# A graph layer's sorting stage: node products added by VectorE from PSUM instead of by GpSimd, the bias added by a matmul later

## The chip, the core and the metric

The kernel runs on one core of a Trainium2 chip. The metric is device time in microseconds. Five engines work in parallel, each through its own in-order queue: TensorE (PE in the profile; its weight loads are the row PEld), VectorE (DVE), ScalarE (ACT), GpSimd (POOL) and SyncE (SP, which only issues DMAs here). They wait for each other by semaphores.

## What is computed

Four steps, each added to the running `x` of 6250 nodes by 256 features:

```
x = x + gnn0(layernorm(x), src, dst, edge_weight)
x = x + ffn0(layernorm(x))          # 8 experts, all used, weighted by a softmax
x = x + gnn1(layernorm(x), src, dst, edge_weight)
x = x + ffn1(layernorm(x))          # 32 experts, one per node

gnn0:  h   = x @ weight_l
       agg = segment_sum(edge_weight[:, None] * h[dst], src)   # 100000 edges
       out = agg + bias_l + x @ weight_r + bias_r
```

The change is in gnn0. The node's own product `x @ weight_r` and the two biases have nothing to do with the edges; `h` is stored and gathered by edge.

## The kernel before, in words

The nodes lie in 49 tiles of 128 rows, and `X` (128 x 49 x 256, f32) holds the running `x` on chip throughout. The program has three stages.

**The sorting stage** (lines 385 to 591, the first 390 us). The edges come sorted by `dst`, but gnn0 sums by `src`. So they are sorted on chip, in 25 groups of 32 edges per partition. The loop at the end of the excerpt below runs over the groups. `count_group(g)` compares each edge's tile number with all 49 (`hot`, DVE), and PE counts by triangular matrices into `count`; ACT copies that into `start`. `place_group(g)` works out each edge's place (DVE: `same`, `picked`, `pos`, `place_b`), makes one-hot rows `to` (L523) and payloads `loads`: four slices by DVE (L527), the fifth by ACT in 32 small instructions (L502), here called pieces. 32 matmuls then move the payloads to their places (`put`, L530); ACT copies `put` to `there` (L533), and POOL assembles `Z` from it with five small instructions. `settle_group(g)` carries the counts to the next group (L482 to L488).

The node products ride along, two tiles per group. `center0` takes mean and variance on DVE, the square root and the centering on ACT (`xn`). `products0` turns `xn` on PE, ACT copies the turned tile to `nT` (L341), and one product of 512 columns gives both `x @ weight_l` and `x @ weight_r` in one PSUM bank `ph` (L570). ACT copies both halves, scaled, to `hs` (L571). A DMA of SP stores the left half as `h0`; POOL adds the right half to `X` (L572), and then the bias (L573).

**Layer 0** (to about 1850 us) interleaves the gather and sum of gnn0 (`aggregate0`: 18 columns of edges per tile; POOL's indirect DMA L201, ACT and DVE weight the rows, L230 and L231, PE sums them in `acc`, L701, DVE adds both halves of `acc` to `X`, L704) with ffn0. **Layer 1** does the same for gnn1 and ffn1, with line L277 as its sum and the one-hot rows of L222 made from `dl_c`, the edge list's local destinations.

Within a stage the order of each engine's queue is not written out: a planner of the framework fixes it when the program is built, from the order in the source, the dependencies and its own idea of durations. `tc.issue_after(ins)` makes the instructions in its block come behind `ins` on the same engine. Buffers limit how far an engine can run ahead: `loads`, `to`, `put`, `ph` and `hs` have two each, `hot` three.

Two biases and their sum: `bias0` (L190 to L192) is loaded by two DMAs on ACT's queue and summed by POOL, in the source before the iotas that make POOL's tables (L430 to L446).

Of the kernel before, what the change touches and what calls it, by code (L numbers as in the profile page):

```python
# [49 lines left out]
def gnn_ffn_kernel(ctx: ExitStack, tc: tile.TileContext, a, out):  # L50
# [56 lines left out]

    src_c = const.tile([P, NCOL], I32, name="src_c")
    val_c = const.tile([P, NCOL], F32, name="val_c")
    dl_c = const.tile([P, NCOL], F32, name="dl_c")  # L110

    bads = [const.tile([P, 1], F32, name=f"bad{i}") for i in range(2)]
    badis = [const.tile([P, 1], I32, name=f"badi{i}") for i in range(2)]
# [73 lines left out]
    wlr = early.tile([P, 2, 2, D], F32, name="wlr")  # L187
    nc.scalar.dma_start(wlr[:, :, 0, :], a["L0_gnn_weight_l"].rearrange("(k p) d -> p k d", p=P))
    nc.scalar.dma_start(wlr[:, :, 1, :], a["L0_gnn_weight_r"].rearrange("(k p) d -> p k d", p=P))
    bias0 = across("L0_gnn_bias_l", early)  # L190
    bias0r = across("L0_gnn_bias_r", early)
    nc.gpsimd.tensor_add(bias0, bias0, bias0r)  # L192
    bias1 = across("L1_gnn_bias")
    br0 = across("L0_ffn_br")
    br1 = across("L1_ffn_router_b")
# [249 lines left out]
    sizes = early.tile([P, NT, NG], F32, name="sizes")  # L445
    nc.gpsimd.memset(ZJ[:, :, NG], 0.0)  # L446

    def count_group(g):


        cs = slice(g * GC, (g + 1) * GC)
        tg = tb[:, cs].rearrange("p (b c) -> p b c", c=4)
        hot = early.tile([P, CB, NT, 4], BF, tag="hot", name="hot", bufs=3)
        nc.vector.tensor_tensor(hot, tg[:, :, None, :].to_broadcast([P, CB, NT, 4]),
                                which_t[:, None, :, :].to_broadcast([P, CB, NT, 4]), OP.is_equal)

        four = early.tile([P, 4, NT, 4], BF, tag="four", name="four", bufs=1)
        nc.vector.tensor_tensor(four, hot[:, :4], hot[:, 4:], OP.add)
        mine = early.tile([P, 4, NT, 2], BF, tag="mine", name="mine", bufs=2)
        nc.vector.tensor_tensor(mine, four[:, :, :, :2], four[:, :, :, 2:], OP.add)  # L460

        count = psum.tile([P, 4, NT], F32, tag="count", name="count", bufs=1)
        base = base_of.pop()
        nc.tensor.matmul(count, row, base[:, None, :].to_broadcast([P, 4, NT]), start=True, stop=True,
                         skip_group_check=True)
        for i in range(2):
            nc.tensor.matmul(count, tri, mine[:, :, :, i], start=False, stop=True, skip_group_check=True)
            for u in range(3):
# [3 lines left out]
        nc.scalar.activation(start, count[:, :, :, None].to_broadcast([P, 4, NT, 4]), AF.Copy)  # L472
        for i in range(2):
            nc.tensor.matmul(count[:, 3, :], rest_tri, mine[:, 3, :, i], start=False, stop=True, skip_group_check=True)
# [13 lines left out]
        nc.vector.scalar_tensor_tensor(full_of[0], total, float(P), full, op0=OP.is_ge, op1=OP.add)  # L488
        nc.gpsimd.tensor_sub(sizes[:, :, g], total, base)

    def place_group(g, hot, start):

        cs = slice(g * GC, (g + 1) * GC)

# [4 lines left out]
        nc.vector.tensor_tensor(same, same, ahead[:, None].to_broadcast([P, 4, 8, 8]), OP.mult)  # L499
        loads = early.tile([P, NPAY, CB, NT, 4], BF, tag="loads", name="loads", bufs=2)  # L500
        for c in range(GC):
            nc.scalar.activation(loads[:, NPAY - 1, c // 4, :, c % 4], hot[:, c // 4, :, c % 4], AF.Copy,  # L502
                                 scale=last[:, g * GC + c:g * GC + c + 1])
# [34 lines left out]
        nc.gpsimd.tensor_add(some[:, 1], there[:, 2], there[:, 3])  # L538
        nc.gpsimd.tensor_add(Z[:, 1, :, g], some[:, 1], there[:, 4])

    def center0(tiles):

        n = len(tiles)
        mv = work.tile([P, NB, 2], F32, tag="mv", name="mv")
        for j, t in enumerate(tiles):
            st = work.tile([P, 6], F32, tag="st", name="st", bufs=4)
            nc.vector.bn_stats(st, X[:, t, :])
            nc.vector.bn_aggr(mv[:, j, :], st)
        std = work.tile([P, NB], F32, tag="std", name="std", bufs=3)
        nc.vector.tensor_scalar(std[:, :n], mv[:, :n, 1], LN_EPS, None, op0=OP.add)  # L550
        shift = work.tile([P, NB], F32, tag="shift", name="shift")
        nc.vector.tensor_scalar(shift[:, :n], mv[:, :n, 0], -1.0, None, op0=OP.mult)
        nc.scalar.activation(std[:, :n], std[:, :n], AF.Sqrt)
        xn = early.tile([P, 2, D], F32, tag="xn0", name="xn0", bufs=2)
        for j, t in enumerate(tiles):
            nc.scalar.activation(xn[:, j, :], X[:, t, :], AF.Identity, bias=shift[:, j:j + 1])
        return tiles, xn, std

    def products0(tiles, xn, std):

        n = len(tiles)
        rstd = work.tile([P, NB], F32, tag="rstd0", name="rstd0")
        nc.vector.reciprocal(rstd[:, :n], std[:, :n])
        hs = early.tile([P, 2, 2, D], F32, tag="hs", name="hs", bufs=2)
        for j, t in enumerate(tiles):
            nT = early.tile([P, 2, P], F32, tag="nT", name="nT", bufs=2)
            transposed(psum, xn[:, j, :], nT)
            ph = psum.tile([P, 2, D], F32, tag="mm", name="ph", bufs=2)
            for k in range(2):
                nc.tensor.matmul(ph, nT[:, k, :], wlr[:, k], start=(k == 0), stop=(k == 1))  # L570
            nc.scalar.activation(hs[:, j], ph, AF.Copy, scale=rstd[:, j:j + 1])  # L571
            nc.gpsimd.tensor_add(X[:, t, :], X[:, t, :], hs[:, j, 1, :])  # L572
            nc.gpsimd.tensor_add(X[:, t, :], X[:, t, :], bias0)  # L573
# [61 lines left out]
    with tc.tile_pool(name="layer0", bufs=1) as wp, tc.tile_pool(name="outs0", bufs=1, side="right") as wo_pool, \  # L635
# [56 lines left out]
        def aggregate0():  # L692
            for b, tiles in enumerate(blocks0):
                idx, dl, w = edges[b]
                for i, t in enumerate(tiles):
                    acc = psum.tile([P, 2, D], F32, tag="agg", name="acc", bufs=2)
                    for j in range(EW):
                        if j % SJ == 0:
                            s = one_hots(wp, dl[:, i, :], j, 3)
                        m = weighted(wp, h0, idx[:, i, j:j + 1], w[:, i, j:j + 1], 12, 6)  # L700
                        nc.tensor.matmul(acc, s[:, j % SJ, :], m, start=(j == 0), stop=(j == EW - 1))  # L701
                        if j == EW - 1:
                            for half in range(2):
                                nc.vector.tensor_add(X[:, t, :], X[:, t, :], acc[:, half, :])  # L704
                        yield
# [404 lines left out]
```

## Time and profile before

| what | value |
|---|---|
| median of 3 runs | 2901.26 us (2896.87 to 2902.55) |
| the profiled execution | 2895.13 us, its span 2893.4 us |
| busy, whole span | PE 93%, DVE 70%, POOL 67%, ACT 56% |
| granted PE clock, whole span | 0.974 |
| POOL's L572, 49 instructions | 78.9 us, mean 1611 ns |
| POOL's L573, 49 instructions | 52.0 us, mean 1060 ns |
| ACT's L571, 49 instructions of 128x512 | 33.7 us, mean 687 ns |
| ACT's L502, 800 instructions | 206.4 us, mean 399 ns |

A line such as L572 is line 572 of the kernel. In a group row the columns are line, engine, operation, names written and read, shapes, count, then busy time and mean, then the idle time of the engine before these instructions and what ended it. In a timeline the columns are start and duration in us. Consecutive instructions of one engine overlap in the record: the time that one really costs its engine is better read from its start to the next start than from its duration.

### The profile page before, as it was taken

Reading aid. Unit: us, or ns where it says so; the run is one execution under the profiler, and the core shown is the slowest. Engines: PE = TensorE matmul, PEld = TensorE weight load, DVE = VectorE, ACT = ScalarE, POOL = GpSimd, SP = SyncE. Lnnn points to the kernel's source line nnn. Section 1 sums busy time; section 2 is a strip of 40 time slices with the busy share of each in tenths; the row PEclk is TensorE's granted clock in tenths of the full one; section 3 lists DMA queues with packets and bytes.
Section 4 is the critical chain, followed back from the end, with each engine's and each line's share of the span. In section 5 each row is a group of like instructions: output and inputs, shape, how many; then the busy total and the mean of one; then the engine's idle time right before and its main releaser. Section 6 shows DMA issues by size and latency. Waiting matters only on the chain.

```text
span 2893.4 us, 37030 instructions
## 1 busy us (share of the span) xinstructions
PE 2677.7 (93%) x10336; PEld 1750.2 (60%) x10336; DVE 2012.4 (70%) x4917; ACT 1626.1 (56%) x3790; POOL 1926.1 (67%) x1932
## 2 busy tenths in 40 slices
PE   5888848888999999999999998779999999999998
PEld 2444427665566666666666665556666666666666
DVE  8999977778768767766566555666666666666630
ACT  6777737655555555555555545455555555555532
POOL 4666667777767676766675527677777777777720
PEclk9999978999999999999999999999999999999999
DMA  4000043333333333333332214333333333333310
GB/s 150 19 19 19 19 141 97 101 100 102 92 99 95 90 101 97 91 100 96 91 102 82 78 39 135 109 108 103 107 108 109 106 108 102 108 106 109 109 44 12
DMA packets 123140, 260.73 MB, mean 90 GB/s; under 512 B 32236, under 2 KB 68904, under 8 KB 122920
## 3 DMA queue, kind: packets, MB, share of 16 engines
q0 software_dynamic: 79872, 218.21, 26.2%
q1 hardware_dynamic: 31672, 32.42, 3.4%
q10 hardware_dynamic: 11376, 7.60, 0.8%
q8 instruction: 85, 1.39, 0.2%
q14 instruction: 135, 1.11, 0.1%
HBM read 238.87 MB, written 19.25 MB: 89 GB/s over the span
## 4 chain that ended last, share of the span: by engine, by line
PE 65%; DVE 17%; DMA 8%; issue 4%; ACT 4%; POOL 1%; ACTq 0%; POOLq 0%; DVEq 0%
PE ph L748 19%; PE py L760 10%; PE py L1000 9%; PE ph L984 9%; PE acc L701 6%; PE acc L277 4%; DMA g<-h,src_c 4%; DMA g<-h,idx 3%; DVE loads L527 3%; DVE to L523 2%; DVE m L231 2%; ACT m L230 2%; PE ph L987 1%; PE ph L214 1%; POOL g L201 1%
## 5 line engine op out<-in xcount | busy, mean ns | idle before, releaser
L201 POOL DMA_INDIRECT g<-h,idx x882 | 903.1, 1024 | 391.8 <-DVE m L231 175.2
L201 POOL DMA_INDIRECT g<-h,src_c x718 | 725.6, 1011 | 227.8 <-issue 104.2
L230 ACT ACTIVATE m<-g,w 128x256 fp32r<-128x256 f32 x882 | 394.7, 500 | 260.0 <-PE acc L701 136.0
L751 ACT ACTIVATE hT<-ph,shift,scale 128x512 f32<-128x512 f32 (+3 forms) x480 | 329.0, 696 | 314.6 <-PE ph L748 313.4
L230 ACT ACTIVATE m<-g,val_c 128x256 fp32r<-128x256 f32 x718 | 349.7, 503 | 273.6 <-PE acc L277 132.2
L231 DVE SCALAR_TENSOR_TENSOR m<-g,val_c,m 128x256 fp32r<-128x256 f32 x718 | 337.1, 483 | 211.2 <-ACT m L230 207.6
L231 DVE SCALAR_TENSOR_TENSOR m<-g,w,m 128x256 fp32r<-128x256 f32 x882 | 397.7, 476 | 42.5 <-ACT m L230 41.4
L748 PE MATMUL ph<-nT,w 128*128 128x512 f32 (+3 forms) x960 | 373.1, 524 | 25.0 <-ACT hT L751 24.8
L760 PE MATMUL py<-wo,hT 128*128 128x256 f32 x1568 | 382.1, 387 | 13.8 <-DVE X L762 10.5
L1000 PE MATMUL py<-w,hm 128*128 128x256 f32 x1568 | 386.7, 385 | 3.1 <-ACT hm L989 3.1
L701 PE MATMUL acc<-m,s 128*128 128x512 f32 x882 | 341.4, 490 | 38.0 <-DVE scale L657 24.7
L984 PE MATMUL ph<-nT,w 128*128 128x512 f32 (+2 forms) x832 | 374.8, 571 | 0.0
L748 PE MATMUL ph<-hT,w 128*128 128x512 f32 (+3 forms) x960 | 368.5, 518 | 0.5 <-ACT hT L751 0.5
L760 PEld LDWEIGHTS py<-wo,hT 128*128 128x128 f32 x1568 | 294.7, 193 | 80.8 <-DVE X L762 26.9
L277 PE MATMUL acc<-m,s 128*128 128x512 f32 x782 | 332.2, 499 | 1.7 <-DVE m L231 1.7
L1000 PEld LDWEIGHTS py<-w,hm 128*128 128x128 f32 x1568 | 292.1, 193 | 52.9 <-ACT hm L989 4.6
L222 DVE TENSOR_TENSOR s<-col,dl 128x384 fp32r<-128x384 f32 x294 | 161.4, 551 | 187.0 <-PE acc L701 184.8
L748 PEld LDWEIGHTS ph<-nT,w 128*128 128x128 f32 x960 | 175.2, 195 | 174.2 <-issue 118.1
L989 ACT ACTIVATE hm<-ph,b 128x512 f32<-128x512 f32 (+2 forms) x208 | 136.8, 659 | 200.0 <-PE ph L987 199.6
L748 PEld LDWEIGHTS ph<-hT,w 128*128 128x128 f32 x960 | 176.2, 193 | 118.9 <-issue 88.3
L701 PEld LDWEIGHTS acc<-m,s 128*128 128x128 f32 x882 | 169.7, 195 | 109.8 <-issue 48.9
L984 PEld LDWEIGHTS ph<-nT,w 128*128 128x128 f32 x832 | 157.2, 191 | 101.5 <-issue 81.1
(248 smaller groups left out, 3359.0 us busy)
## 6 DMA issues: line engine op xcount, KB each, us to landing
g<-h,idx POOLq DMA_INDIRECT x882, 2.8
g<-h,src_c POOLq DMA_INDIRECT x718, 2.8
h<-hs SPq DMA_DIRECT2D x25, 256.0 KB, 2.1
X<-in_x_dram SPq DMA_DIRECT2D x12, 512.0 KB, 8.9
out_dram<-o SPq DMA_DIRECT2D x11, 512.0 KB, 3.4
h<-hs SPq DMA_DIRECT2D x9, 512.0 KB, 3.0
w<-in_L_ffn_W_dram ACTq DMA_DIRECT2D x2, 2048.0 KB, 11.2
wo<-in_L_ffn_Wo_dram ACTq DMA_DIRECT2D x1, 2048.0 KB, 20.0
```

What stands on the lines that cost most here:

```text
L201: nc.gpsimd.indirect_dma_start(out=g, out_offset=None, in_=h, in_offset=bass.IndirectOffsetOnAxis(ap=idx, axis=0))
L222: nc.vector.tensor_tensor(s[:, :n], col[:, None, :].to_broadcast([P, n, P]), dl[:, j:j + n, None].to_broadcast([P, n, P]), OP.is_equal)
L230: nc.scalar.activation(m[:, 0, :], g, AF.Copy, scale=w)
L231: nc.vector.scalar_tensor_tensor(m[:, 1, :], g, w, m[:, 0, :], op0=OP.mult, op1=OP.subtract)
L277: nc.tensor.matmul(acc, s[:, (j - js.start) % SJ, :], m, start=opens, stop=done)
L701: nc.tensor.matmul(acc, s[:, j % SJ, :], m, start=(j == 0), stop=(j == EW - 1))
L748: nc.tensor.matmul(ph[:, :nw], (w1, w2)[layer][:, e, k, m * P:(m + 1) * P], src[:, k, :nw], start=(k == 0), stop=(k == 1))
L751: nc.scalar.activation(hT[:, m, :nw], ph[:, :nw], AF.Relu, bias=shift[:, layer, c:c + 1], scale=scale[:, layer, c:c + 1])
L760: nc.tensor.matmul(py, hT[:, k, j * P:(j + 1) * P], wo[:, e, k, :], start=(k == 0), stop=(k == 1))
L984: nc.tensor.matmul(ph[:, :nw], w1f[:, k, c * P:(c + 1) * P], nT[:, k, :nw], start=(k == 0), stop=False)
L989: nc.scalar.activation(hm[:, :nw], ph[:, :nw], AF.Relu, bias=b1[:, c:c + 1])
L1000: nc.tensor.matmul(py[:, j, :], now[:, cols], w2f[:, c, :], start=False, stop=(c == NC1 - 1), skip_group_check=True)
```

## The change

The right half of a product is no longer evicted by ACT. DVE multiplies it, in PSUM, by the reciprocal deviation and adds it to `X` in one instruction; ACT evicts only the left half, so `hs` has half its size. POOL's two additions per tile are gone. The bias is added in layer 0: on `acc`, behind the first of a tile's 18 products, a further product of `ones_b` (three rows of ones, else zero) and `bias0_b` (the bias split in three bf16 parts on those rows). POOL makes these behind its tables. The mean and variance of a group's tiles (`stats0`) are taken one group earlier than before, and the reciprocal moves from `products0` to `center0`. In `place_group` the pieces 16 to 31 are made to follow ACT's last eviction of `products0` of the same group. `dl_c` becomes bf16 (its values are 0 to 127, or those plus 8192).

```diff
-    dl_c = const.tile([P, NCOL], F32, name="dl_c")
+    dl_c = const.tile([P, NCOL], BF, name="dl_c")
...
-    bias0 = across("L0_gnn_bias_l", early)
-    bias0r = across("L0_gnn_bias_r", early)
-    nc.gpsimd.tensor_add(bias0, bias0, bias0r)
+    bias0 = across("L0_gnn_bias_l", prep)
+    bias0r = across("L0_gnn_bias_r", prep)
...
     nc.gpsimd.memset(ZJ[:, :, NG], 0.0)
 
+    nc.gpsimd.tensor_add(bias0, bias0, bias0r)
+    bias0_b = const.tile([P, D], BF, name="bias0_b")
+    nc.gpsimd.memset(bias0_b, 0.0)
+    ones_b = const.tile([P, P], BF, name="ones_b")
+    nc.gpsimd.memset(ones_b, 0.0)
+    for i in range(3):
+        own = slice(32 * i, 32 * i + 1)
+        nc.gpsimd.memset(ones_b[own, :], 1.0)
+        for _ in range(i):
+            nc.gpsimd.tensor_copy(bias0_b[own, :], bias0[own, :])
+            nc.gpsimd.tensor_sub(bias0[own, :], bias0[own, :], bias0_b[own, :])
+        nc.gpsimd.tensor_copy(bias0_b[own, :], bias0[own, :])
...
-    def place_group(g, hot, start):
+    def place_group(g, hot, start, evicted):
...
         for c in range(GC):
-            nc.scalar.activation(loads[:, NPAY - 1, c // 4, :, c % 4], hot[:, c // 4, :, c % 4], AF.Copy,
-                                 scale=last[:, g * GC + c:g * GC + c + 1])
+
+            with ExitStack() as behind:
+                for ins in evicted[-1:] if c >= GC // 2 else ():
+                    behind.enter_context(tc.issue_after(ins.ins))
+                nc.scalar.activation(loads[:, NPAY - 1, c // 4, :, c % 4], hot[:, c // 4, :, c % 4], AF.Copy,
+                                     scale=last[:, g * GC + c:g * GC + c + 1])
...
-    def center0(tiles):
+    def stats0(tiles):
...
         nc.scalar.activation(std[:, :n], std[:, :n], AF.Sqrt)
+        return tiles, std, shift
+
+    def center0(tiles, std, shift):
+
+        n = len(tiles)
+        rstd = work.tile([P, NB], F32, tag="rstd0", name="rstd0")
+        nc.vector.reciprocal(rstd[:, :n], std[:, :n])
         xn = early.tile([P, 2, D], F32, tag="xn0", name="xn0", bufs=2)
         for j, t in enumerate(tiles):
             nc.scalar.activation(xn[:, j, :], X[:, t, :], AF.Identity, bias=shift[:, j:j + 1])
-        return tiles, xn, std
-
-    def products0(tiles, xn, std):
+        return tiles, xn, rstd
+
+    def products0(tiles, xn, rstd):
...
-            nc.scalar.activation(hs[:, j], ph, AF.Copy, scale=rstd[:, j:j + 1])
-            nc.gpsimd.tensor_add(X[:, t, :], X[:, t, :], hs[:, j, 1, :])
-            nc.gpsimd.tensor_add(X[:, t, :], X[:, t, :], bias0)
-        nc.sync.dma_start(h0[tiles[0] * P:(tiles[0] + n) * P, :].rearrange("(t p) d -> p t d", p=P), hs[:, :n, 0, :])
+            evicted.append(nc.scalar.activation(hs[:, j], ph[:, 0, :], AF.Copy, scale=rstd[:, j:j + 1]))
+            nc.vector.scalar_tensor_tensor(X[:, t, :], ph[:, 1, :], rstd[:, j:j + 1], X[:, t, :],
+                                           op0=OP.mult, op1=OP.add)
+        nc.sync.dma_start(h0[tiles[0] * P:(tiles[0] + n) * P, :].rearrange("(t p) d -> p t d", p=P), hs[:, :n, :])
+        return evicted
...
     counted = count_group(0)
-    centered = center0(pairs[0])
+    measured = stats0(pairs[0])
+    centered = center0(*measured)
+    measured = stats0(pairs[1])
     settle_group(0, *counted[2:])
     for g in range(NG):
...
-        products0(*tiles0)
-        place_group(g, *now[:2])
+        evicted = products0(*tiles0)
+        place_group(g, *now[:2], evicted)
         if g + 1 < NG:
-            centered = center0(pairs[g + 1])
+            centered = center0(*measured)
+            if g + 2 < NG:
+                measured = stats0(pairs[g + 2])
             settle_group(g + 1, *counted[2:])
...
                         nc.tensor.matmul(acc, s[:, j % SJ, :], m, start=(j == 0), stop=(j == EW - 1))
+                        if j == 0:
+                            nc.tensor.matmul(acc[:, 0, :], ones_b, bias0_b, start=False, stop=False,
+                                             skip_group_check=True)
```

More of the change, by code (lines that the diff above doesn't have):

```diff
@@ L550, in center0 @@
         nc.vector.tensor_scalar(std[:, :n], mv[:, :n, 1], LN_EPS, None, op0=OP.add)
-        shift = work.tile([P, NB], F32, tag="shift", name="shift")
+        shift = work.tile([P, NB], F32, tag="shift", name="shift", bufs=3)
         nc.vector.tensor_scalar(shift[:, :n], mv[:, :n, 0], -1.0, None, op0=OP.mult)
         nc.scalar.activation(std[:, :n], std[:, :n], AF.Sqrt)
+        return tiles, std, shift
[3 more added lines that the diff above has]
+        nc.vector.reciprocal(rstd[:, :n], std[:, :n])
         xn = early.tile([P, 2, D], F32, tag="xn0", name="xn0", bufs=2)
@@ L556, in center0 @@
             nc.scalar.activation(xn[:, j, :], X[:, t, :], AF.Identity, bias=shift[:, j:j + 1])
-        return tiles, xn, std
-    def products0(tiles, xn, std):
+        return tiles, xn, rstd
+    def products0(tiles, xn, rstd):
         n = len(tiles)
-        rstd = work.tile([P, NB], F32, tag="rstd0", name="rstd0")
-        nc.vector.reciprocal(rstd[:, :n], std[:, :n])
-        hs = early.tile([P, 2, 2, D], F32, tag="hs", name="hs", bufs=2)
+        hs = early.tile([P, 2, D], F32, tag="hs", name="hs", bufs=2)
+        evicted = []
         for j, t in enumerate(tiles):
```

## The prediction

> **What bounds the kernel now.** I read the table of busy time by stretch first, to find the stage that the change touches and its limit. Columns: stretch, length, busy us (and instructions) of PE, PE's weight load, DVE, ACT and POOL, granted clock, DMA share, GB/s.
>
> ```profile
> 82.90:368.40 285.50, 249.29 (x1100) 126.91 (x1101) 285.14 (x622) 226.97 (x840) 183.76 (x200) 1.00 0.06 19
> 450.00:1850.00 1400.00, 1342.40 (x4922) 885.01 (x4921) 986.16 (x2499) 793.09 (x1558) 944.69 (x925) 0.98 0.33 95
> ```
>
> The first row is the steady part of the sorting stage, 20 groups of 14.28 us: DVE is busy in all of it. The second is layer 0, where PE is busy 96%. Next I read the timelines of DVE and POOL over one group (start, duration), then the same DVE lines in the first groups, while POOL is not adding.
>
> ```profile
> 183.16 0.73 DVE L484 TENSOR_SCALAR wrap<-total 128x49 f32<-128x49 f32 x1
> 183.99 0.68 DVE L486 TENSOR_TENSOR base_of<-total,wrap 128x49 bf16<-128x49 f32 x1
> 185.55 0.88 DVE L497 TENSOR_TENSOR same<-tq 128x256 bf16<-128x256 bf16 x1
> 183.11 0.73 POOL L573 TENSOR_TENSOR X<-X,L_gnn_bias_l_b 128x256 f32<-128x256 f32 x1
> 183.80 0.80 POOL L572 TENSOR_TENSOR X<-X,hs 128x256 f32<-128x256 f32 x1
> ```
>
> ```profile
> 47.72 0.18 DVE L484 TENSOR_SCALAR wrap<-total 128x49 f32<-128x49 f32 x1
> 24.45 0.21 DVE L486 TENSOR_TENSOR base_of<-total,wrap 128x49 bf16<-128x49 f32 x1
> 21.82 0.40 DVE L497 TENSOR_TENSOR same<-tq 128x256 bf16<-128x256 bf16 x1
> ```
>
> DVE's L484 ends at 183.89, POOL's add that it overlaps at 183.84; L486 ends at 184.67, POOL's at 184.60. DVE is standing still behind POOL's additions, and the profile counts that as busy. From start to next start the excess in a group is 0.55 (L484), 0.47 (L486), 0.48 (L497) and 0.35 us (L482, 0.50 against 0.15), **1.85 us together**.
>
> DVE's full row suggests that relieving it is enough. The timelines of PE and ACT over the next group say otherwise.
>
> ```profile
> 196.80 7.38 PE L530 MATMUL put<-loads,to 128*128 128x245 bf16 x32
> 205.87 0.21 PE L474 MATMUL count<-mine,rest_tri 128*128 128x49 bf16 x2 [0.88 <-ACT start L472]
> 209.22 1.98 PE L570 MATMUL ph<-wlr,nT 128*128 128x512 f32 x4 [0.88 <-ACT nT L341]
> 204.27 0.38 ACT L533 ACTIVATE there<-put 128x245 f32<-128x245 f32 x1 [2.90 <-PE put L530]
> 204.54 0.62 ACT L502 ACTIVATE loads<-hot,last 128x49 bf16<-128x49 bf16 x2
> 205.00 0.81 ACT L472 ACTIVATE start<-count 128x784 bf16<-128x784 f32 x1
> 208.21 0.69 ACT L571 ACTIVATE hs<-ph,rstd 128x512 f32<-128x512 f32 x1
> 208.79 0.38 ACT L341 ACTIVATE nT<-tr 128x256 f32<-128x256 f32 x1
> ```
>
> From put to put PE passes twice through ACT: put, eviction `there`, two pieces (L502), `start`, count, first product, eviction `hs`, transpose eviction `nT`, second product, put. No DVE instruction lies in it. After the delayed put at 82.89, PE's own pace shows: the next puts are at 96.92, 111.18 and 125.42. The loop takes **14.24 us** with two pieces ahead of `start`, and 14.03 in the one group that had one (ACT at 90.64). So two loops of nearly the same length run side by side, and the gain is set by the one that shrinks less.
>
> **The change, part by part.** Two rows price the new operations (group row of layer 0; instruction row of layer 1's bias product with min/median/max ns):
>
> ```profile
> L762 DVE SCALAR_TENSOR_TENSOR X<-py,gate,X 128x256 f32<-128x256 f32 x392 | 186.7, 479 | 36.4 <-PE py L760 34.4
> L998 PE MATMUL py<-b,hotT x49: 272/273/285, 1848.0 to 2858.6; 128*128 128x256 bf16 x49
> ```
>
> DVE's loop: POOL's 49+49 additions (L572, L573, 131 us, off the bound) go, and with them the 1.85 us. Two of the operation of L762 come, from PSUM, by the same form: 2 x 0.40 (start to start, as L231) to 2 x 0.48. 14.28 - 1.85 + 0.8 to 1.0 = **13.2 to 13.4 us**. POOL's six small additions per group (L535 to L489) stay; today they lie beside the long L527, at 0.03 us each. If they fall on short operations instead they cost up to 0.5 each; I take nothing here and keep 1 us per group for the range.
>
> Would the new addition be held by POOL too? L762 in layer 0 runs at 479 ns beside a POOL of another kind of work, so the trace has no case. The Trainium skill, "SBUF — State Buffer", section "Who interferes with whom": POOL and DVE lock each other out only if DVE reads two inputs from SBUF or is in a two-port mode. This one reads one tensor from SBUF and one from PSUM, so it escapes. By the rows L484 to L497 alone, up to 0.5 us each and 14.3 again; I go by the rule, because most of POOL's colliding work is gone anyway.
>
> PE's loop: `hs` is halved, 128x512 (687 ns, next start after 0.58) to 128x256. Nearest are L341 (128x256 from PSUM, 372 ns, next start 0.27) and L230 (with a scale, 500 ns, 0.40). Of the two evictions one lies on the loop (ahead of `nT`): -0.18 to -0.31, I take -0.25. The pieces that ACT slips in ahead of `start` cost 0.21 each. Half of a group's pieces may now not come before that group's last `hs`, so fewer are at hand: 0 to -0.42, I take half. 14.24 - 0.25 - 0.21 = **13.78 us**, longer than DVE's. Sixteen pieces behind `hs` end 0.35 + 16 x 0.23 = 4.0 us after it starts; put needs the 17th after 16 x 0.225 = 3.6 us and the 32nd after 7.0, and the 17th is there after 0.7: no wait while only the two `xn` come between. Were that cover gone, put would wait for up to the whole 4 us.
>
> 20 groups x (14.28 - 13.78) = **-10.0 us**.
>
> The first groups: puts at 47.74 and 67.78 are 20.0 apart. ACT ran 11 pieces and `dl_c` ahead of `nT` (PE idle 2.59 at 59.11), PE's clock then halved (3.78 for a product of 1.98), and DVE's reciprocal waited 3.40 at 71.56 for a square root behind 12 pieces. Half of those pieces are now barred, and the square root belongs to a group earlier: -6 to 0, I take **-4**; part of the 20 is the edge check, which stays.
>
> The bias pieces: tables (L430 to L446) no longer wait 9.37 us behind the bias DMA (L192), which frees about 1.1 us of DVE (L183 at 12.40, next start after 1.44, against 0.9; L184 1.09 against 0.5). Behind them come nine one-partition copies and differences, at most 0.73 each (L573 unhindered) beside a full DVE: -1.1 to +6.6. DVE meets POOL only in part: **+1**. DMAs on ACT's queue are the same two; SP's `h0` stores keep 256 KB and now wait for ACT alone.
>
> Layer 0: 49 bias products. L998 is the same form; the timeline has its start at 2378.33 and the next at 2378.44, so 0.109 us each, 49 x 0.109 = **+5.3 us** on a busy PE. Zero where PE was waiting for `m` anyway, 49 x 0.2 = 10 if the weight load (98 ns, then 190) shows. The bf16 `dl_c` meets an f32 `col` in L222, off the bound; like L675, which mixes the two: nothing.
>
> **Sum**: -10.0 - 4 + 1 + 5.3 = -7.7. The profiled execution took 2895.1 (span 2893.4 and 1.7 around it), so 2887.4; it lies 6.1 below the median 2901.26, which gives **2893.5 us**.
>
> **The wait that is added.** DVE's addition needs the product, and stands in DVE's in-order queue; behind it stand `to`, for which put waits, and `hot`. The rule that speaks against the change: the Trainium skill, "PSUM — Partial Sum Buffer", section "PSUM bank collisions raise a hardware error": ScalarE and VectorE must not read one bank at once, even at other columns. Both halves of `ph` lie in one bank, so the addition must wait for `hs` also, about 0.5 us more; no row here shows two engines on one bank. Without it, the second addition could start at 196.9; by it, at 197.4. Today `to` starts at 194.47. Behind `to` the addition costs DVE an idle moment that its 0.4 us of slack and the next wait absorb; I count no loss.
>
> **Rivals.**
> 1. *PE's loop gives only the shorter eviction* (the two pieces stay): 20 x 0.29 = -5.8, no gain in the first groups, +1, +5.3: +0.5, 2902. For: ACT has spare pieces of the next group. Against: the 14.03 group.
> 2. *Both loops open*, PE overlapping count with put, DVE's 13.25 the bound: -20.6 - 4 + 1 + 5.3 = -18.3, 2883.
> 3. *Slower: the second addition is queued ahead of `to`.* Then put follows the product by 0.5 (eviction) + 0.48 + 2.2 (`to`) = 3.2 us: 13.78 + 3.2 = 17.0, 20 x 2.7 = +54, with -4, +1, +5.3 about +56, 2957. It decides from the point where the addition stands ahead of `to` at all. For: the order is fixed before the run, and ACT's order (12 pieces, then 2.90 us idle for put) shows that a shorter put was reckoned with, so PE was thought early. Against: `to` starts 2.9 us before the addition can.
> 4. *Small losses*: DVE's idle behind `to` not absorbed, or POOL falling on short operations, 0.5 us x 20 more than counted, or 10 in layer 0: 2906 to 2920.
>
> **Chances.** Forecast 0.36, rival 2 0.12, rival 1 0.20, rival 3 0.17, rival 4 0.15. A change below 0.2% (5.8 us) is about what a measurement of this kernel cannot tell from none. Faster: 0.48; same: 0.20; slower: 0.32. The forecast's own range is 2884 to 2899 (PE's loop 13.5 to 14.0, the bounds above). The range to record, 2876 to 2938, leaves out most of rival 3 (0.15) and 0.05 below.
>
> **What would show it.** Right: L484, L486, L497 at 0.18, 0.21, 0.40 in every group; DVE with gaps; puts 13.5 to 14.0 apart; `hs` at 0.4; puts 2 and 3 nearer than 20; bias products 0.11 from start to start. Wrong: PE idle at L530 for `to` with DVE idle for ACT's `hs`; ACT waits inside put; Z's additions stretched and DVE full again.

## The result, and the profile after

The changed kernel takes **2940.53 us** (median of 4 runs, 2939.55 to 2945.67) against 2901.91 us (4 runs, 2896.87 to 2904.01) for the kernel before: a ratio of **1.0148**, 95% interval 1.0133 to 1.0163, so 38.6 us slower. The forecast was 2893.5. The measured time lies 2.5 us above the upper end of the range, on the side of rival 3.

I read the profile after in the order of the prediction. First the table of busy time by stretch, with the columns as before: the same 20 groups (by the starts of their puts), and 1400 us of layer 0.

```profile
87.00:401.10 314.10, 245.90 (x1103) 128.30 (x1101) 262.10 (x652) 219.86 (x854) 42.65 (x120) 0.91 0.05 18
475.00:1875.00 1400.00, 1340.38 (x4932) 877.54 (x4932) 985.73 (x2491) 791.73 (x1549) 952.53 (x915) 0.98 0.33 94
```

DVE was busy for 285.14 us of 285.50; now for 262.10 of 314.10. The work that was to go has gone: 23 us of DVE's, and most of POOL's. But the 20 groups take 28.6 us longer. So somebody waits who did not wait before. PE's granted clock over these groups is 0.91 instead of 1.00, but the 32 matmuls of a put still take 7.36 to 7.41 us in 19 of them, and a product that runs unbroken 1.96 or 1.98, as before, so the clock is not what lengthens the groups. The view of waits over these groups names both ends (engine and line that wait, what for; total, times, longest):

```profile
DVE X L594 <- ACT hs L593: 51.9, 29, 3.7
PE put L546 <- DVE to L539: 42.6, 18, 4.0
```

The timeline of DVE over two groups shows how the two hang together. L594 is the new addition, L539 is `to`:

```profile
206.71 0.48 DVE L594 SCALAR_TENSOR_TENSOR X<-ph,rstd,X 128x256 f32<-128x256 f32 x1 [3.33 <-ACT hs L593]
209.52 0.48 DVE L594 SCALAR_TENSOR_TENSOR X<-ph,rstd,X 128x256 f32<-128x256 f32 x1 [0.17 <-ACT hs L593]
210.83 2.28 DVE L539 TENSOR_TENSOR to<-place_b,which_q 128x4096 bf16<-128x4096 bf16 x1
...
223.81 0.48 DVE L594 SCALAR_TENSOR_TENSOR X<-ph,rstd,X 128x256 f32<-128x256 f32 x1 [1.54 <-ACT hs L593]
225.12 2.27 DVE L539 TENSOR_TENSOR to<-place_b,which_q 128x4096 bf16<-128x4096 bf16 x1
227.31 0.48 DVE L594 SCALAR_TENSOR_TENSOR X<-ph,rstd,X 128x256 f32<-128x256 f32 x1
```

In the first of these groups both additions stand ahead of `to` in DVE's queue, in the second only the first one does. PE and ACT over the same time:

```profile
203.83 1.96 PE L592 MATMUL ph<-wlr,nT 128*128 128x512 f32 x4
207.00 1.98 PE L592 MATMUL ph<-wlr,nT 128*128 128x512 f32 x4 [0.90 <-ACT nT L340]
213.16 7.38 PE L546 MATMUL put<-loads,to 128*128 128x245 bf16 x32 [3.97 <-DVE to L539]
227.45 2.87 PE L546 MATMUL put<-loads,to 128*128 128x245 bf16 x12 [1.14 <-DVE to L539]
```

```profile
203.80 0.62 ACT L518 ACTIVATE loads<-hot,last 128x49 bf16<-128x49 bf16 x2
204.26 0.81 ACT L484 ACTIVATE start<-count 128x784 bf16<-128x784 f32 x1
206.21 0.46 ACT L593 ACTIVATE hs<-ph,rstd 128x256 f32<-128x256 f32 x1
206.57 0.37 ACT L340 ACTIVATE nT<-tr 128x256 f32<-128x256 f32 x1
209.02 0.47 ACT L593 ACTIVATE hs<-ph,rstd 128x256 f32<-128x256 f32 x1
```

Read it as one chain. The second product ends at 208.98; `hs` evicts its left half; the addition starts at 209.52, 0.54 behind the product; then come DVE's `over`, reciprocal, statistics and `place_b` until 210.83; `to` takes 2.28; put starts at 213.16. That is 4.18 us from product to put, with PE idle for 3.97 of it. In the group with one addition ahead, put waits 1.14. The starts of the puts are therefore **17.12 and 14.28 us** apart in turn, from the seventh put to the 23rd; the mean of the 20 groups is 15.70. Ten pairs of groups lose 10 x (17.12 - 14.28) = 28.4 us against a steady 14.28.

The short instructions are as short as the prediction had them, in every group (group rows of DVE over these groups: count, busy us, mean ns, idle before):

```profile
L594 DVE SCALAR_TENSOR_TENSOR X<-ph,rstd,X 128x256 f32<-128x256 f32 x41 | 19.8, 483 | 52.0 <-ACT hs L593 51.9
L509 DVE TENSOR_TENSOR same<-tq 128x256 bf16<-128x256 bf16 x20 | 8.4, 418 | 0.0
L498 DVE TENSOR_TENSOR base_of<-total,wrap 128x49 bf16<-128x49 f32 x19 | 4.1, 215 | 0.0
L496 DVE TENSOR_SCALAR wrap<-total 128x49 f32<-128x49 f32 x20 | 3.8, 188 | 0.0
```

The additions themselves take 19.8 us; the idle time ahead of them is 52.0.

**Where the 38.6 us are.** Starts of the first, fourth and last put: 37.80, 87.00 and 413.5, before 33.6, 82.9 and 381.6. So +4.2 at the first put, nothing more to the fourth, +28.6 in the 20 groups after it. The first tile sum of layer 0 ends 31.0 us later than before. From the 16th to the 49th tile the distance grows by 4.4 us, 0.13 for each of 33 tiles; taken for all 49 bias products that is 6.4, an estimate. With the 31.0 that makes 37.4. The group row of these products (count, busy us, mean ns, idle before):

```profile
L730 PE MATMUL acc<-bias_b,ones_b 128*128 128x256 bf16 x49 | 13.9, 284 | 0.0
```

The mean of 284 ns is a duration; in the sum of a tile each is worth 0.13, since matmuls overlap in the record.

The profiled executions are 50.5 us apart (2945.67 and 2895.13), because the one lies 5.1 above its median and the other 6.8 below; the rest of what the two traces differ by, some 6 us in the first 15 tiles and 7 behind the last, is about as much as that scatter of 11.9, and I make nothing of it. Since these 13 us are left out, that 37.4 comes so near to 38.6 is no test of the sum.

### The profile page after: what moved, and what is told of

It reads as the page before. It is cut to its first block, busy times and chain, and to the rows that moved or that the text cites. A ratio compares the mean times of both kernels' runs of the same rounds, so it can differ in the third digit from the quotient of the medians.

```text
span 2943.8 us, 36996 instructions
## 1 busy us (share of the span) xinstructions
PE 2690.3 (91%) x10385; PEld 1751.7 (60%) x10385; DVE 1992.7 (68%) x4966; ACT 1615.7 (55%) x3790; POOL 1787.1 (61%) x1848
## 4 chain that ended last, share of the span: by engine, by line
PE 66%; DVE 10%; DMA 10%; ACT 6%; issue 5%; POOL 2%; ACTq 0%; SPq 0%; POOLq 0%; DVEq 0%
PE ph L778 18%; PE py L790 10%; PE py L1030 8%; PE ph L1014 8%; PE put L546 6%; PE acc L728 5%; DMA g<-h,src_c 5%; PE acc L276 4%; DMA g<-h,idx 4%; ACT loads L518 2%; DVE m L230 2%; POOL g L200 2%; DVE to L539 2%; ACT m L229 1%; PE ph L1017 1%
## 5 line engine op out<-in xcount | busy, mean ns | idle before, releaser
L200 POOL DMA_INDIRECT g<-h,idx x882 | 920.9, 1044 | 386.0 <-DVE m L230 167.9
L778 PEld LDWEIGHTS ph<-nT,w 128*128 128x128 f32 x960 | 175.3, 196 | 175.3 <-issue 118.2
L546 PE MATMUL put<-loads,to 128*128 128x245 bf16 x800 | 186.3, 405 | 55.6 <-DVE to L539 55.6
```

What stands on the lines that cost most here:

```text
L200: nc.gpsimd.indirect_dma_start(out=g, out_offset=None, in_=h, in_offset=bass.IndirectOffsetOnAxis(ap=idx, axis=0))
L546: nc.tensor.matmul(put, to[:, c // 4, :, c % 4], loads[:, :, c // 4, :, c % 4], start=(c == 0), stop=(c == GC - 1))
L778: nc.tensor.matmul(ph[:, :nw], (w1, w2)[layer][:, e, k, m * P:(m + 1) * P], src[:, k, :nw], start=(k == 0), stop=(k == 1))
```

## The experiments

They ran on three other chips of the kind. There the kernel before takes 3277 to 3282 us, and repeated runs of a kernel spread by over 1%. The difference lies behind the sorting stage: the changed kernel's puts come at the same times (last one at 413.7 on one of these chips, and 413.5 on the first). So I compare ratios to the kernel before on the same chip, and the puts. The expectations call the prediction's part on DVE's loop step 1, that on PE's loop step 2, and the prices of the small parts step 3.

**The changed kernel again.**

> The changed kernel itself, on the chip of the other three runs, so that the shares have one ground. A ratio of 1.0148 to the kernel before was measured: 1.010 to 1.017 here. The order of the sorting stage does not depend on the chip: periods of 14.28 and 17.12 us in turn, last put within 1 us of 413.5.

3314.08 us, ratio 1.0093 (1.0070 to 1.0115), 4 runs; periods of 14.29 and 17.12 us in turn, last put 413.7. The next four runs were on another chip than this one, so only ratios and puts join them. The order of the stage is a property of the program. The share is just under the expected one, 30.5 us (23 to 38) instead of 38.6; whether layers 0 and 1, which are slower there, take up part of the delay is not shown.

**Both additions behind `to`.** Only their place in DVE's queue changes; the pieces stay barred.

```diff
-            nc.vector.scalar_tensor_tensor(X[:, t, :], ph[:, 1, :], rstd[:, j:j + 1], X[:, t, :], ...)
+            own_of.append((ph, rstd, j, t))
...
-        nc.vector.tensor_tensor(to, ...)
+        placed = nc.vector.tensor_tensor(to, ...)
+        with tc.issue_after(placed.ins):
+            for ph, rstd, j, t in own_of:
+                nc.vector.scalar_tensor_tensor(X[:, t, :], ph[:, 1, :], rstd[:, j:j + 1], X[:, t, :], ...)
```

> The changed kernel with one thing moved: VectorE's two additions out of PSUM are emitted behind `to` of the same group, and held there by issue_after. Theory 1 (the additions stand too far forward in VectorE's queue; VectorE waits up to 3.33 us for `hs`, and `to` and put wait behind it): VectorE's wait for `hs` is gone or under 0.5 us a group, puts are 13.1 to 13.8 us apart in every group instead of 14.28 and 17.12 in turn, the last put starts at 372 to 385 us instead of 413.5, and the whole takes 2898 to 2912 us. Theory 2 (ScalarE's 16 barred pieces hold `nT` and so TensorE): puts stay over 15 us apart on average, total over 2930. Theory 3 (the loss is in layer 0, by the bias product): the sorting stage shrinks, but the total stays over 2925.

3244.58 us, ratio **0.9916** (0.9885 to 0.9946), 8 runs: faster than both kernels. The periods are 13.2 to 13.4 from the sixth on, the last put is at 361.3, 11 us earlier than even Theory 1 expected. DVE, PE (two timelines), and the busy time over 223 us of the stage:

```profile
188.40 2.33 DVE L539 TENSOR_TENSOR to<-place_b,which_q 128x4096 bf16<-128x4096 bf16 x1
190.65 0.86 DVE L543 SCALAR_TENSOR_TENSOR X<-ph,rstd,X 128x256 f32<-128x256 f32 x2
```

```profile
190.78 7.38 PE L550 MATMUL put<-loads,to 128*128 128x245 bf16 x32 [0.17 <-DVE to L539]
```

```profile
112.00:335.00 223.00, 206.72 (x927) 106.41 (x926) 223.00 (x557) 180.80 (x705) 92.01 (x102) 0.99 0.06 20
```

The additions follow `to` with no idle time ahead of them, put waits 0.17, and DVE is full again, at 13.3 us a group. That the loss of the changed kernel in its groups comes from the place of the additions is shown: the same instructions in another order lose nothing. Against this kernel the place costs more than against the one before: the last put is 52 us later (413.5 and 361.3), since the groups of 14.28 lose 1 us each too.

**No piece held back**, and nothing else changed: the additions are left where the planner puts them.

```diff
-                for ins in evicted[-1:] if c >= GC // 2 else ():
-                    behind.enter_context(tc.issue_after(ins.ins))
```

> The changed kernel with only the bar on the pieces taken away: all 32 pieces of a group may be issued at any time, the additions stay where the planner puts them. Theory 1: the additions still stand ahead of `to`, and `hs` now also comes later behind more pieces: the same as the changed kernel or slower, 2935 to 2965. Theory 2: it recovers most of the loss, under 2915.

3269.13 us, ratio 0.9982 (0.9952 to 1.0013), 12 runs: no difference from the kernel before, and the loss of the changed kernel is gone. The periods are 13.9 and even, the last put is at 387.5. Theory 1, by which the bar on the pieces has no part in the loss, missed. Theory 2 had the size, but not for its reason, since the run above loses nothing with the bar in place. DVE without the bar:

```profile
191.38 2.27 DVE L536 TENSOR_TENSOR to<-place_b,which_q 128x4096 bf16<-128x4096 bf16 x1
196.26 0.48 DVE L591 SCALAR_TENSOR_TENSOR X<-ph,rstd,X 128x256 f32<-128x256 f32 x1 [0.58 <-ACT hs L590]
197.14 0.48 DVE L591 SCALAR_TENSOR_TENSOR X<-ph,rstd,X 128x256 f32<-128x256 f32 x1
205.26 2.27 DVE L536 TENSOR_TENSOR to<-place_b,which_q 128x4096 bf16<-128x4096 bf16 x1
```

Counted through the queues, both additions still stand ahead of `to` of their own group, in every group. But from the third put on PE makes the products a group ahead of the put (eight whole tile products stand before the third put, five in the changed kernel). So the additions come behind the `to` of the put that follows these products (191.38), and are done 7.6 us before the next `to` (205.26). What costs is therefore an addition ahead of a `to` whose put comes right behind the addition's own product. The bar and the additions are not two independent parts of the change: taking a bar off ACT's instructions moved PE's products, and with them the additions. How the planner came to either order is not shown.

The period of 13.9 is PE's own loop. Its first product stands behind `start` here (it starts at 204.55, behind the count, which waited 0.89 us for ACT), and put waits for nothing of DVE's. This is close to the state that was forecast, 13.78. The kernel doesn't gain because its start is bad: the first four puts are at 42.1, 57.6, 80.0 and 98.1, 15 us late by the fourth. At the second put the products are not yet a group ahead; an addition waits 6.3 us for `hs`, and put 6.5 for `to`.

**Both**: additions behind `to`, and no piece held back.

> As behind_to, and the pieces 16 to 31 need not follow `hs` any more. Theory 1: the pieces' order is a side matter; puts 13.1 to 14.3 us apart, total within 10 us of behind_to. Theory 2: this one is faster than behind_to by over 20 us.

3245.22 us, ratio 0.9890 (0.9850 to 0.9930), 4 runs. Periods about as with the bar, 13.2 to 13.3; the fourth put is at 80.6 (83.5 with the bar), the last at 357.6. The two kernels can't be told apart by their times.

**POOL's bias addition alone taken away**: the kernel before with its bias by the product in layer 0 (and `dl_c` in bf16), its other addition and its evictions as they were.

```diff
-            nc.gpsimd.tensor_add(X[:, t, :], X[:, t, :], bias0)
...
+                        if j == 0:
+                            nc.tensor.matmul(acc[:, 0, :], ones_b, bias0_b, start=False, stop=False, ...)
```

> The kernel before with only the bias moved: GpSimd makes the bf16 parts behind its tables, layer 0 adds them by a product, GpSimd adds only the own product to X; dl_c is bf16; everything else of the sorting stage as before. Theory 1: layer 0 gains 49 x 0.11 = 5 us; the sorting stage loses one of the two collisions with GpSimd but TensorE's loop of 14.24 us holds, so the last put stays within 3 us of 381.6; total 2903 to 2912. Theory 3: total 2915 to 2925, with the last put unmoved.

3277.71 us, ratio 0.9985 (0.9958 to 1.0013), 12 runs. Periods 14.25; the last put is at 377.6, 4.0 us earlier and so 1 more than expected, 2.4 of it gained at the third put. The busy time over 223 us, in the kernel before and here:

```profile
112.00:335.00 223.00, 194.74 (x869) 99.35 (x866) 222.64 (x484) 176.49 (x653) 143.76 (x156) 1.00 0.06 20
112.00:335.00 223.00, 194.23 (x865) 100.29 (x863) 205.77 (x486) 177.50 (x656) 113.80 (x125) 1.00 0.06 19
```

DVE got 17 us back, about 1.1 a group, and the groups are as long as they were to 0.04 us.

**Both of POOL's additions taken away**: the kernel before without L572 and L573, so that the own product and the bias of layer 0 are missing from its result.

> The kernel before without POOL's 98 additions; the own product and the bias of layer 0 are then left out of the result. Step 1 of the prediction: DVE's loop loses 1.85 us of its 14.28, leaving 12.4. Step 2 said that PE's own loop through ACT, 14.24 us with the whole 128x512 eviction, binds next to it. If step 2 is right the periods of the puts stay at 14.1 to 14.3 and the time is within 5 us of the kernel before. If DVE alone sets the period and PE's loop has room, 12.4 to 13.2, and the time is 22 to 40 us below the kernel before (ratio 0.988 to 0.993).

3270.02 us, ratio 0.9958 (0.9935 to 0.9981), 16 runs. Periods 14.19 to 14.21, as step 2 had it; the last put is at 377.7. The time is further below the kernel before than the 5 us expected, by 14 us (6 to 21), of which the sorting stage shows 4; where the rest lies is not shown. Busy time, then PE's puts, then DVE's reciprocal:

```profile
112.00:335.00 223.00, 195.20 (x869) 100.85 (x867) 198.99 (x487) 177.05 (x658) 89.65 (x94) 1.00 0.06 20
```

```profile
195.40 7.37 PE L530 MATMUL put<-loads,to 128*128 128x245 bf16 x32
209.59 2.65 PE L530 MATMUL put<-loads,to 128*128 128x245 bf16 x11
```

```profile
197.78 0.17 DVE L563 RECIPROCAL rstd<-std 128x2 f32<-128x2 f32 x1 [1.56 <-ACT std L553]
```

DVE has 24 us to spare and sits idle for ACT's square root; put doesn't wait for DVE at all, and its period is PE's own. That is step 2's reading of the profile of before, tested on its own: in a kernel whose DVE row is full, a DVE that is relieved is worth 0.08 us a group (14.28 to 14.20).

**The statistics back in one piece**: the kernel with the additions behind `to`, with `stats0` and `center0` joined as before, so that the centred tile does not come a group earlier.

```diff
-    def stats0(tiles):
+    def center0(tiles):
...
-            centered = center0(*measured)
-            if g + 2 < NG:
-                measured = stats0(pairs[g + 2])
+            centered = center0(pairs[g + 1])
```

> The changed kernel with its two additions held behind the placement compare of their own group (as in the run of that name, whose periods were 13.2 to 13.3 with DVE full), and with the statistics back in one piece with the centred tile, as before, so that the centred tile does not come a group earlier. If the split is what shortened PE's loop below the predicted 13.78 (PE can transpose for the next group ahead of the put), the periods are 13.7 to 14.3 and last put 370 to 385. If PE's loop had that room anyway, and DVE's 13.3 is the bound with and without the split: 13.2 to 13.4, last put 356 to 363.

3283.95 us, ratio 1.0017 (0.9997 to 1.0037), 20 runs. Periods of 15.30 and 14.22, in turn or nearly, 15.0 in the mean of the 20 groups, the last put at 395.6: above both expectations. Two things happen (lines of ACT, DVE and PE):

```profile
185.63 3.82 ACT L518 ACTIVATE loads<-hot,last 128x49 bf16<-128x49 bf16 x16
189.29 0.19 ACT L573 ACTIVATE std<-std 128x2 f32<-128x2 f32 x1
```

```profile
189.51 0.17 DVE L583 RECIPROCAL rstd<-std 128x2 f32<-128x2 f32 x1 [0.88 <-ACT std L573]
```

```profile
195.46 0.21 PE L486 MATMUL count<-mine,rest_tri 128*128 128x49 bf16 x2 [1.11 <-ACT start L484]
195.73 1.98 PE L591 MATMUL ph<-wlr,nT 128*128 128x512 f32 x4
```

The square root stands behind the 16 barred pieces, and the reciprocal waits for it with the group's placement work behind it in DVE's queue; put then waits for `to`, up to 0.9 us, in 7 of some 15 groups. And PE's first product stands behind `start` again (195.46, then 195.73), as in the kernel before; in the changed kernel it runs at 203.83, beside the eviction `there`, because its `nT` was made while put ran (198.84). In the groups without a wait for `to` PE's loop takes 14.22, as before the change. So with the bar in place, both losses come back with the statistics in one piece; without the bar the split was not undone.

**The bias products left out**: the changed kernel without its 49 products, so the bias is missing from the result.

> The changed kernel without its 49 bias products in layer 0; the bias of layer 0 is then left out of the result. Sorting stage as in the changed kernel (last put 413.5 within 1 us). Step 3 priced the products at 49 x 0.109 = 5.3 us: 4 to 7 us below the changed kernel on the same chip. Rival: the changed kernel's layers 0 and 1 ran 13 to 20 us longer than before behind the last put; if the bias products are the cause of all of that (a product of another weight between two of the tile sum, with its weight load shown), 12 to 20 us below. If PE waits for the gathered rows in layer 0 anyway: 0 to 2 us below.

3303.58 us (10 runs), ratio 1.0082 (1.0055 to 1.0108), against 1.0093 (1.0070 to 1.0115) with them. The puts agree to 0.1 us. The difference of the two ratios, 0.0011 or 3.6 us, is less than either's uncertainty: this run can't tell 5 us from 0 or from 12. The 0.13 us a tile above remains the only measure.

**Own and left product in two PSUM banks**, in the changed kernel.

```diff
+            pr = psum.tile([P, 2, D], F32, tag="mr", name="pr", bufs=2)
             for k in range(2):
-                nc.tensor.matmul(ph, nT[:, k, :], wlr[:, k], ...)
+                nc.tensor.matmul(ph[:, 0, :], nT[:, k, :], wlr[:, k, 0], ...)
+            for k in range(2):
+                nc.tensor.matmul(pr[:, 1, :], nT[:, k, :], wlr[:, k, 1], ...)
```

> The changed kernel with the left and the own product in two PSUM banks, made by twice as many 128x256 products. In the changed kernel both additions wait for ScalarE's eviction of the same bank, 0.5 us behind the product. If that wait belongs to the shared bank, the additions now wait for PE's product, and the long groups shrink by 0 to 0.5 us. The additions stay ahead of the placement compare by the order written out, so the loss stays: mean period 15.2 to 16.0, last put 400 to 420. If the shared bank, not the place in the queue, was the cause: periods 13.2 to 14.3 in all groups.

3351.20 us, one run; periods 16.0 to 19.1 from the fifth put on, mean 17.1, last put 446.7: beyond the expected 15.2 to 16.0. Timelines of PE, ACT and DVE:

```profile
204.72 1.03 PE L595 MATMUL pr<-wlr,nT 128*128 128x256 f32 x4
209.38 2.07 PE L593 MATMUL ph<-wlr,nT 128*128 128x256 f32 x4 [3.41 <-ACT nT L340]
```

```profile
205.29 3.82 ACT L518 ACTIVATE loads<-hot,last 128x49 bf16<-128x49 bf16 x16
```

```profile
205.79 0.48 DVE L597 SCALAR_TENSOR_TENSOR X<-pr,rstd,X 128x256 f32<-128x256 f32 x1 [0.27 <-PE pr L595]
207.10 2.28 DVE L539 TENSOR_TENSOR to<-place_b,which_q 128x4096 bf16<-128x4096 bf16 x1
```

The addition now starts 0.04 us behind its product (204.72 + 1.03 = 205.75) instead of 0.54, and waits for PE, no longer for ACT. So the wait for `hs` came with the shared bank. But the planner ordered all queues anew, and the loss is another one. Both additions stand ahead of their `to` in nearly every group, yet put does not wait for `to` (it ends at 209.38, put starts at 211.25). Put stands behind a product, and this product waits 3.41 us for its `nT`, which ACT makes at 208.95, behind its 16 barred pieces. So the run neither prices the bank nor tests the additions' place; it shows that the bar can hold PE through `nT`, as Theory 2 had it, in another order of the queues.

**POOL kept adding**: additions behind `to`, no piece held back, and eight needless POOL additions per group.

```diff
+            twice = early.tile([P, D], F32, tag="twice", name="twice", bufs=1)
+            for _ in range(4):
+                nc.gpsimd.tensor_add(twice, hs[:, j], hs[:, j])
```

> The kernel with the additions behind the placement compare and no pieces held back, and eight needless POOL additions 128x256 f32 per group beside it (twice = hs + hs, behind each eviction of a left product). By the rule that step 1 relied on (a DVE instruction that reads one tensor from SBUF and one from PSUM is not held by POOL) the own additions stay at 0.45 to 0.50 us while POOL adds beside them, and DVE's two-input instructions on SBUF next to them grow by 0.3 to 0.6 us for each POOL addition that they meet: up to 8 x 0.5 = 4 us a group, periods of 14 to 17.5. If the rule does not hold for this form: own additions of 0.7 to 1.2 us. If there is no such lock: periods 13.2 to 13.4 as without.

3314.60 us, one run; periods 15.35 and 16.0, mean 15.7, where the kernel without the eight has 13.3. POOL, then DVE beside it:

```profile
211.58 4.86 POOL L597 TENSOR_TENSOR twice<-hs 128x256 f32<-128x256 f32 x6
```

```profile
211.41 0.86 DVE L540 SCALAR_TENSOR_TENSOR X<-ph,rstd,X 128x256 f32<-128x256 f32 x2
...
213.01 0.61 DVE L496 TENSOR_SCALAR wrap<-total 128x49 f32<-128x49 f32 x1
...
213.72 0.61 DVE L498 TENSOR_TENSOR base_of<-total,wrap 128x49 bf16<-128x49 f32 x1
...
215.14 0.83 DVE L509 TENSOR_TENSOR same<-tq 128x256 bf16<-128x256 bf16 x1
```

While POOL adds, the two own additions take 0.86 us together, as without it, and the instructions on SBUF next to them take 0.61, 0.61 and 0.83 where the changed kernel has 0.19, 0.21 and 0.42. That is the stretch that the prediction read from the profile of before, made at will; and the form that reads `ph` from PSUM escapes it.

**The bias pieces after group 5**, in the kernel with additions behind `to` and no bar.

```diff
-    nc.gpsimd.tensor_add(bias0, bias0, bias0r)
...
         if g == 1:
             check_edges()
             prep_ctx.close()
+        if g == 5:
+            nc.gpsimd.tensor_add(bias0, bias0, bias0r)
...
```

> The changed kernel with both additions behind the placement compare of their group, no pieces held back, and POOL's bias pieces made after group 5 instead of ahead of group 0. In the kernel with the pieces in front the first put came at 35.5 and the last at 357.6. If the nine copies and differences of POOL stretched DVE's start (step 3, bias pieces +1), the first put comes 0.5 to 3 us earlier, last put 354.5 to 357, and the time is 1 to 3 us below that kernel. If the first put is late for another reason (half of the next group's product ahead of it in PE's queue): first put unchanged within 0.3, no difference, and the pieces cost one later group up to 4 us.

3243.39 us, ratio 0.9905 (0.9871 to 0.9938), 7 runs. First put at 34.4, last at 356.4, against 35.4 and 357.8 with the pieces in front, in the same kernel beside it:

> The same kernel as the earlier run of that name (ratio 0.989 to before), beside the one with the later bias pieces on one chip: ratio 0.985 to 0.993, periods 13.2 to 13.3, last put within 1 us of 357.6.

3242.66 us, ratio **0.9904** (0.9868 to 0.9941), 6 runs. The pieces cost 1.0 us at the first put, as step 3 had it (+1); the times can't tell the two apart.

## Why the prediction was wrong, step by step

**What bounds the kernel: right.** Two loops of nearly the same length. Without POOL's additions DVE has 24 us of 223 to spare and the period goes only from 14.28 to 14.20.

**DVE's loop, 13.2 to 13.4: right.** With the additions behind `to`, DVE is full at 13.3. Of the terms, the stretch is gone from the rows; by DVE's busy time with and without POOL's additions (222.64 and 198.99 of 223) it was worth 1.6 us a group, not 1.85. The addition takes 0.40 us from its start to the next (206.71 to 207.11; 0.40 to 0.48 estimated). The Trainium skill, "SBUF — State Buffer", section "Who interferes with whom", was taken against the rows L484 to L497, which would have given 14.3; the run with POOL kept adding bears it out, at 0.86 us for the two additions.

**PE's loop, 13.78: too long, by a term that was left out.** The shorter eviction gave 0.21 (start of `hs` to start of `nT`, 0.37 instead of 0.58) where I took 0.25. The two pieces ahead of `start` stayed two in the changed kernel (203.80), where I took one. What I missed is the split of the statistics: with it the first product can come from behind `start` to beside `there`. In the changed kernel the second product ends at 208.98, 12.94 us after the put at 196.04 (a transposition of 0.2 us from start to next start comes ahead of the next put), and the run with the statistics in one piece shows 14.22 without it. The split alone is not enough: in the run with no piece held back the first product stood behind `start`, at 13.9. With the additions out of the way this loop is under DVE's 13.3, so the state that I called rival 2 (period 13.25) is what the change can do.

**The wait that is added: this is the step that failed.** "I count no loss" assumed that the second addition stands behind `to`, because `to` started 2.9 us before the addition could. That compares two times of a trace with an order that is fixed before any time is known. In the changed kernel's steady groups both additions stand ahead of `to` in every other group, and one in the rest; put waits 3.97 and 1.14 us for `to`, where I had nothing. Rival 3 had the mechanism and the place. That its long period of 17.0 meets the measured 17.12 is luck: two errors cancel. The chain from product to put takes 4.18 us (I had 3.2, leaving out `over`, the reciprocal, the statistics and `place_b` between addition and `to`), on a loop that is shorter (12.94, not 13.78). It was also wrong in the number of groups: 10 instead of 20, so +28.4 instead of +54. The argument for it, that the order is fixed before the run and a shorter put was reckoned with, was already in the text; the argument against it says nothing about an order.

**The shared bank**: that the addition waits for the eviction of its bank was taken from the Trainium skill, "PSUM — Partial Sum Buffer", section "PSUM bank collisions raise a hardware error". The addition starts 0.54 us behind the product (0.5 estimated), and 0.04 with two banks. Whether the chip needs this wait is not shown: the program sets it.

**The pieces put ahead or behind**: no put of the changed kernel's steady groups waits for a piece, as worked out. That the bar acts on the order of PE's products and DVE's additions was not seen at all.

**First groups, -4, and bias pieces, +1: of the wrong sign in the changed kernel**, +4.2 at the first put. There PE's queue has half of the next group's product ahead of the first put, and its `nT` stands behind the 16 barred pieces on ACT (lines of ACT and PE):

```profile
31.85 3.82 ACT L518 ACTIVATE loads<-hot,last 128x49 bf16<-128x49 bf16 x16
35.50 0.38 ACT L340 ACTIVATE nT<-tr 128x256 f32<-128x256 f32 x1
```

```profile
35.93 2.08 PE L592 MATMUL ph<-wlr,nT 128*128 128x512 f32 x2 [4.28 <-ACT nT L340]
37.80 0.41 PE L546 MATMUL put<-loads,to 128*128 128x245 bf16 x1
```

The wait of "up to the whole 4 us" that I priced for the 16 pieces is here, at another victim: `nT`, which I did not list behind them. Without the bar, and the additions behind `to`, the fourth put is 2.3 us earlier than before (80.6), near the -3 of the sum.

**Bias products, +5.3**: 0.13 us a tile and 6.4 in all by the trace, of the predicted size; the run without them could not resolve it. `dl_c` at nothing was not tested by itself.

**The sum**: steady groups -10.0, measured +28.6; first groups with the bias pieces -3, measured +4.1; the last period and the way to the first tile sum 0, measured -1.7; bias products +5.3, measured 6.4. The measured terms give 37.4, beside the 38.6. With the additions behind `to` the last put comes 20 us earlier than before (361.3), and 24 without the bar too (357.6); rival 2 is built on such groups. A slip in the range: the least term named in rival 4, 0.5 us x 20 more than the forecast, gives 2903.5, not the 2906 at which it starts.

## What to carry to other kernels

When a change gives an engine an instruction that waits for a late result, ask first where it stands in that engine's queue and what stands behind it; if a planner sets the order, a trace of the kernel before can't answer, so hold the instruction behind the one on the critical path explicitly. A bar on one engine's queue is not local: here, with it, an addition of another engine stood where it cost 2.84 us in every second group; without it, PE's products ran a group ahead and the additions cost nothing there. And before relieving a full engine, look for a second loop of the same length: taking 24 us of 223 from DVE alone was worth 0.08 us a group.

## What the runs showed that was not expected

- The lock between DVE and POOL costs POOL too. In the run with the eight additions, POOL's subtraction L501 takes 0.28 us in one group and 2.34 in the one before, where it ends 0.14 us behind DVE's `to` (208.96 + 2.53 = 211.49); `to` itself took 2.28 in the changed kernel. Lines of POOL and of DVE:

```profile
209.29 2.34 POOL L501 TENSOR_TENSOR sizes<-total,base_of 128x49 f32<-128x49 f32 x1
...
223.85 0.28 POOL L501 TENSOR_TENSOR sizes<-total,base_of 128x49 f32<-128x49 f32 x1
```

```profile
208.96 2.53 DVE L536 TENSOR_TENSOR to<-place_b,which_q 128x4096 bf16<-128x4096 bf16 x1
```

That whichever of the two started first keeps the other waiting is how I read it; it was not tested by itself.
- The profile counts DVE's standing still as busy time, and the loss does not show as a wait anywhere: in the kernel before DVE was "busy" for 222.64 us of 223, of which 17 went with one of POOL's two additions.
- Twice as many products of half the width cost nothing noticeable: with two banks, eight products of 128x256 take 1.84 us from their first start to the transposition behind them (203.75 to 205.59), and four of 128x512 take 1.82 in the changed kernel (207.00 to 208.82).
